# Queries and keys of twelve heads by two nested levels of seven block products, for both batch elements at once

## The chip, the cores and the metric

The kernel runs on one core of a Trainium2 chip. The metric is the device time of one execution in microseconds (us), as the median of several runs. Engines are named as the profile names them: PE (TensorE, matrix products; PEld is its weight load), DVE (VectorE), ACT (ScalarE), POOL (GpSimd) and SP, the queue from which nearly all DMAs are issued.

## The reference

A decoder layer in float32 on two batch elements of 512 tokens with 512 features. It has self-attention, cross-attention, a gated feed-forward part, and a layer normalisation after each.

```python
# self-attention: 16 heads of 128; the weights are FP4 codes with a scale per 32 rows
q = x @ (wq_codes * rows(wq_scales)) + bq          # k and v likewise
scores = einsum('bqhd,bkhd->bhqk', q, k) / sqrt(128)
out = einsum('bhqk,bkhd->bqhd', softmax(scores), v)
x = layernorm(x + out @ (wo_codes * rows(wo_scales)) + bo)
# cross-attention on 1024 context rows, of which the 54 best scores are kept
scores = where(scores < top_k(scores, 54)[..., -1:], -inf, scores)
x = layernorm(x + (softmax(scores) @ ctx) @ W_o.T)
# feed-forward: 512 -> 2 x 2048 -> 512
x = layernorm(x + (silu(gate) * up) @ w_down.T)
```

## The kernel before

**Block products.** Most products are done by a seven-product scheme for 2 x 2 blocks in place of eight: sums and differences of the blocks are formed first (`combine_a` for the stationary side, `combine_b` for the moving side, four operations each), then seven products run on TensorE, and their results are added up. `seven` does this for one block product: it numbers its products 1 to 7, gathers products 1, 6 and 7 in one PSUM bank `r`, from which ScalarE keeps three copies `u` (with the bias), and products 2, 4, 5, 3 in a two-bank PSUM tile `z`. Two VectorE operations form the results: `on_second` reads `z` and `u` before product 3 runs, `on_first` after it. The rest of a `seven` (product 3 and `on_first`) is left open, and is closed inside the next one. There are two buffers of `r`, two of `z` and two of one-bank tiles of the tag `t`; the scores of a head take both `z`.

**Units and phases.** A unit is one head of one element: 32 units. A phase is a group of four heads (`GH = 4`) of one element: eight phases. A phase has one product block for its values (`values`, two `seven`), one for its part of the output projection (`project`, two `seven`, added to the residual), and its four units. Before the change the first four heads are done for both elements, then the rest of the first element, then the rest of the second:

```python
phases = [(0, 0), (0, 1)] + [(g, b) for b in range(B) for g in range(1, NG)]
half_way = (NG + 1) * GH
```

**A unit.** `queries_keys(u)` makes queries and keys by one `seven` with 14 products of 128x256 (seven, two chunks of 128 features each). `weights(u)` computes the scores (four 128x512 products), the row maxima on VectorE, exponentials and scaling on ScalarE, a 32x32 transpose of four tiles on VectorE into `tq`, and then sixteen DMAs from SP that finish the transpose into `pt`. `attend(u)` multiplies `pt` by the values. In the main loop, step `i` makes queries, keys and weights of unit `i + 2` and attends unit `i`.

**Weights.** Codes and scales of a head's queries and keys are loaded (`load_qk`, `load_scales`), multiplied on GpSimd (`dequantise`, two pieces) and combined (`combine_qk`); values and output weights likewise. There are three buffers of scales (`sc0` to `sc2`). Apart from the first four heads, a head's weights are loaded and prepared once for each element.

**The search.** When the first element's self-attention is over (step `half_way`), its normalisation, the turning of its rows (`turn_x`), its cross-attention queries (`xquery`) and scores (`xscores`, steps `XS`) are worked into the second element's steps. The search for the 54th best score (`clips`) is a chain of maxima and replacements on VectorE, four of whose steps are written into each unit from `half_way + 4`.

**Order.** The order of each engine's instructions is made when the program is built. A scheduler takes the instructions by priority, which is the order of the program text, and lets a later one pass when an earlier one isn't ready by its own clock. On the chip each engine then follows its list.

Of the kernel before, what the change touches and what calls it, by code (L numbers as in the profile page):

```python
# [16 lines left out]
P = 128  # L17
# [7 lines left out]
def decoder_layer(  # L25
# [42 lines left out]
    sb = ctx.enter_context(tc.tile_pool(name="sb", bufs=1))  # L68
    ps = ctx.enter_context(tc.tile_pool(name="ps", bufs=2, space=PSUM))


# [173 lines left out]

    def load_residual():

        bo_sb = place("mt0", (D,), "bo_sb")
        nc.sync.dma_start(out=bo_sb, in_=bo.to_broadcast([P, D]))
        for b in range(B):  # L250
            rb[b] = place(f"res{b}", (NT, D), f"res{b}")
            nc.sync.dma_start(out=rb[b], in_=x[b].rearrange("(t p) d -> p t d", p=P))
            for t in range(NT):
                res[b, t] = rb[b][:, t, :]
                nc.gpsimd.tensor_tensor(res[b, t], res[b, t], bo_sb, ALU.add)
# [391 lines left out]

    phases = [(0, 0), (0, 1)] + [(g, b) for b in range(B) for g in range(1, NG)]
    units = [(g, b, j) for g, b in phases for j in range(GH)]
    half_way = (NG + 1) * GH  # L650
    last = len(phases) - 1

    def owner(p):
        return 0 if p == 1 else p

    def place_of_qk(u):

        return (u if u < GH else (u - GH) % 5) if u < half_way else (1, 2, 0)[(u - half_way) % 3]

    qkw, vw, ow, ks, qs, pts, vs, ots, raw = {}, {}, {}, {}, {}, {}, {}, {}, {}  # L660
    parts = {}
    scale_count = [0]

    def load(key, tag, shape, source, scales):

        w = place(tag, shape, "w" + key)
        if source is not None:
            nc.sync.dma_start(out=w, in_=source)
        raw[key] = (w, scales)

    def load_scales(key, n, queue):
        w, scales = raw[key]
        at, sv = scales[n]
        part = w if at is None else w[:, at, :]
        sct = place(f"sc{scale_count[0] % 3}", tuple(part.shape[1:]), f"s{key}_{n}")
        scale_count[0] += 1
        queue.dma_start(out=sct, in_=sv)
        parts[key, n] = (part, part, sct)
# [32 lines left out]
    def combine_qk(eng, u):  # L711
        w = raw[f"qk{owner(u // GH) * GH + u % GH}"][0]
        qkw[u] = combine_a(eng, blocks_pair(w), place(f"wc{u % 2}", (4, HK, P), f"wc{u}"))

    def combine_v(eng, p):
        w = raw[f"v{owner(p)}"][0]
        vw[p] = combine_a(eng, blocks_t(w), place("cmb0", (4, HK, GW // 2), f"vc{p}"))

# [17 lines left out]
    def queries_keys(u):  # L736

        g, b, j = units[u]
        h = g * GH + j
        qt = place(f"q{u % 2}", (2, HS), f"q{u}")  # L740
        kt = place(f"k{u % 2}", (2, HS), f"k{u}")
        seven(
# [8 lines left out]
        )  # L751
        qs[u], ks[u] = qt.rearrange("p n s -> p (n s)"), kt.rearrange("p n s -> p (n s)")

    def first_queries_keys():

        z = double("zqk0", (2, S))
        for k in range(KD):
            for c, n in ((c, n) for c in range(NT) for n in range(2)):
# [8 lines left out]
                )  # L767
        qs[0] = place("q0", (S,), "q0")
        ks[0] = place("k0", (S,), "k0")
        nc.scalar.activation(qs[0], z[:, 0, :], AF.Identity, bias=bq_sb[:, 0:1])  # L770
        nc.scalar.activation(ks[0], z[:, 1, :], AF.Identity, bias=bks[:, 0:1], scale=HSCALE)

    def weights(u):

        q, k = qs.pop(u), ks.pop(u)
        tq = place(f"tq{u % 2}", (NB, NT, NT, BLK), f"tq{u}")
        for t in range(NT):
            if t % 2 == 0:
# [7 lines left out]
                for n in range(2):  # L786
                    nc.tensor.matmul(  # L787
                        pair[n],
                        q[:, (t + n) * P : (t + n + 1) * P],
                        k,  # L790
                        start=True,
                        stop=True,
                    )
# [63 lines left out]
    def combine_o(eng, p):  # L857
        w = raw[f"o{p}"][0]
        ow[p] = combine_a(eng, blocks_t(w), place("wv" if p == last else "cmb1", (4, GH // 2, HD), f"oc{p}"))

    def project(p):

        g, b = phases[p]
        lo, hi = ots.pop((p, 0)), ots.pop((p, 1))
        oc = combine_b(
            nc.vector if p == last else nc.gpsimd,
            (lo[:, :, :HS], lo[:, :, HS:], hi[:, :, :HS], hi[:, :, HS:]),
            place("cmb0", (4, GH // 2, HS), f"otc{p}"),
        )
        rr = rb[b].rearrange("p (h s) (c f) -> p h s c f", h=2, c=2)  # L870
        for s in range(NT // 2):

            def add(z, u, s=s, c=1):
# [9 lines left out]
                oc,  # L883
                ow[owner(p)],
                slice(s * P, (s + 1) * P),
# [51 lines left out]
    combine_qk(nc.gpsimd, 2)  # L937
    dequantise(nc.gpsimd, "qk3")
    load_o(0)
    load_scales("o0", 0, nc.sync)  # L940
    load_scales("o0", 1, nc.sync)
    dequantise(nc.gpsimd, "o0", 0)
    dequantise(nc.gpsimd, "o0", 1)
    combine_o(nc.gpsimd, 0)


    due = {}
    for p in range(2, len(phases)):
        for j in range(GH):
            due.setdefault(p * GH + j - 1, []).append((f"qk{p * GH + j}", 0))  # L950
        for n in range(2):
            due.setdefault(p * GH - 3 + n, []).append((f"v{p}", n))
            due.setdefault((p * GH + 3 if p < last else p * GH + 2) + n, []).append((f"o{p}", n))

# [7 lines left out]
    lag = 2  # L962
    for i in range(len(units)):
        g, b, j = units[i]
        u = i + lag
        if u < len(units):
            gu, bu, ju = units[u]
            if ju == 0:
                values(u // GH)
            queries_keys(u)  # L970
            for key, n in due.get(u, []):
                dequantise(nc.gpsimd, key, n)
                if key == f"qk{u + 1}":
                    combine_qk(nc.gpsimd, u + 1)
                    if ju == GH - 1:
                        combine_v(nc.gpsimd, (u + 1) // GH)
                if key[0] == "o" and n == 1:
                    combine_o(nc.gpsimd, int(key[1:]))
            if u + 1 < 2 * GH:
                combine_qk(nc.gpsimd, u + 1)  # L980
                if u + 1 == GH:
                    combine_v(nc.gpsimd, 1)
        p = i // GH
        if j == 0 and 0 < p < last:
            project(p - 1)
            if p > 1:
                load_o(p)
        if i == len(units) - 2:
# [5 lines left out]
        if u < len(units):  # L994
            weights(u)
            if i == last * GH - 1:
                load_o(last)
            if 2 * GH <= u + 3 < len(units):
                load_qk(u + 3)
            if ju == 0 and 1 < u // GH + 1 < len(phases):  # L1000
                load_v(u // GH + 1)
            for key, n in due.get(u + 1, []):
                load_scales(key, n, nc.sync)
        if i == 0:
            load_residual()
            combine_x(nc.gpsimd, 1, "x0")
        if i == 2 * GH:
            load_memT(0)
# [74 lines left out]
    def up(b, half, eng, search=iter(()), between=iter(()), other=None, at=None):  # L1083
# [25 lines left out]
        for n in range(NH):  # L1109
# [10 lines left out]
            if other and n == (NH - 1 if at is None else at):  # L1120
                for _ in search:
                    pass
                for _ in other:
                    if sums:
                        sums.pop()()
            ut = place(f"k{n % 2}", (2, HS), f"ut{i}_{b}")
            uts[:] = [ut]
# [5 lines left out]

            def first(z, u, i=i, n=n, ut=ut, ht=hs[n]):
                gt = place(f"q{n % 2}", (2, HS), f"gt{i}_{b}")
                nc.vector.tensor_add(gt, z, u)  # L1136
# [175 lines left out]
```

## Time and profile before

| | |
|---|---|
| median of 3 runs | 1082.58 us (1081.91 to 1083.0) |
| the profiled execution | 1082.82 us, span 1081.0 us |
| mean granted TensorE clock | 0.998 |
| PE busy | 1070.0 us (99%), 4300 instructions |
| DVE busy | 610.9 us (57%) |
| POOL busy | 574.3 us (53%) |
| ACT busy | 409.0 us (38%) |
| DMA | 142.72 MB, mean 132 GB/s |

A product in float32 appears as two PE instructions, so `x8` in a row of the profile is four products. PE's busy time is modelled from its instructions' lengths; how far apart their starts are tells more. A group's row ends with the engine's idle time ahead of its instructions and what ended it.

### The profile page before, as it was taken

The page shows a single profiled execution, that of the slowest core. Times are in us where ns is not written, and L with a number is a line of the kernel's source. Part 1 is how long each engine was busy: PE and PEld are TensorE (multiplying, and loading weights), DVE is VectorE, ACT ScalarE, POOL GpSimd, SP SyncE. Part 2 cuts the span into 40 slices and gives each one's busy share as a digit, 9 for nine tenths or more (in the row PEclk, how much of TensorE's full clock was granted, in tenths as well). Part 3 has the DMA queues.
Part 4 walks back from the last instruction along what each step waited for, and adds up shares of the span by engine and source line. Part 5 has one row for each costly group of instructions (what it writes and reads, how often), then busy time and mean ns, then how long its engine had stood idle before and what let it go on. Part 6 is the DMA issues. An engine that isn't in the chain of part 4 may idle for free.

```text
span 1081.0 us, 12892 instructions
## 1 busy us (share of the span) xinstructions
PE 1070.0 (99%) x4300; PEld 801.8 (74%) x4300; DVE 610.9 (57%) x1015; ACT 409.0 (38%) x882; POOL 574.3 (53%) x578
## 2 busy tenths in 40 slices
PE   9999999999999999999999999999999999999997
PEld 7676776677677677665666567778888888888886
DVE  5444334334434435643898774468999736554254
ACT  3445335335344533733444353222443214221221
POOL 4965636846845846514852654525565712264530
PEclk9999999999999999999999999999999999999999
DMA  9545456554663555635442537331324401522201
GB/s 349 160 106 175 156 137 222 178 162 143 192 195 95 175 170 156 196 81 180 136 117 78 146 109 253 88 108 39 97 66 131 136 21 49 166 82 78 96 19 39
DMA packets 66258, 142.72 MB, mean 132 GB/s; under 512 B 12560, under 2 KB 12560, under 8 KB 66192
## 3 DMA queue, kind: packets, MB, share of 16 engines
q1 hardware_dynamic: 65472, 140.32, 42.4%
q10 hardware_dynamic: 720, 1.57, 0.4%
q8 instruction: 35, 0.57, 0.2%
q14 instruction: 31, 0.25, 0.1%
HBM read 99.90 MB, written 2.10 MB: 94 GB/s over the span
## 4 chain that ended last, share of the span: by engine, by line
PE 83%; DVE 13%; ACT 2%; POOL 1%; issue 1%; DMA 0%; DVEq 0%; ACTq 0%; POOLq 0%
PE sc L787 10%; PE av L832 9%; PE zqk L187 9%; PE rqk L187 7%; PE zgu L187 7%; PE zo L187 5%; PE rgu L187 5%; PE zv L187 5%; PE zpd L187 4%; PE ro L187 4%; DVE work L493 4%; PE rv L187 3%; DVE top L496 3%; PE rpd L187 3%; PE zxav L187 3%; PE xs L474 2%
## 5 line engine op out<-in xcount | busy, mean ns | idle before, releaser
L798 DVE TENSOR_REDUCE nm<-sc 128x2 f32<-128x1024 f32 x63 | 77.0, 1223 | 80.1 <-PE sc L787 80.1
L832 PE MATMUL av<-pt,v 128*128 128x512 f32 x256 | 121.6, 592 | 0.0
L787 PE MATMUL sc<-k,q 128*128 128x512 f32 x256 | 117.1, 598 | 0.0
L801 ACT ACTIVATE p<-sc,nm 128x512 f32<-128x512 f32 x128 | 86.9, 681 | 76.0 <-DVE nm L798 75.9
L812 DVE STREAM_TRANSPOSE tq<-p 128x512 f32<-128x512 f32 x128 | 84.9, 699 | 36.9 <-ACT p L809 30.7
L787 PEld LDWEIGHTS sc<-k,q 128*128 128x128 f32 x256 | 47.3, 190 | 62.2 <-issue 51.3
L107 POOL TENSOR_TENSOR wc<-wgu 128x256 f32<-128x256 f32 x32 | 25.4, 794 | 114.8 <-PE zgu L187 70.9
L809 ACT ACTIVATE p<-p,sm 128x512 f32<-128x512 f32 x128 | 85.4, 715 | 1.6 <-DVE sm L808 1.4
L684 POOL TENSOR_TENSOR wqk<-wqk,sqk 128x512 f32<-128x512 f32 x52 | 66.0, 1286 | 35.9 <-DMA wqk<-in_wqk 20.4
L197 ACT ACTIVATE ugu<-rgu 128x256 f32<-128x256 f32 x96 | 36.3, 379 | 103.1 <-PE rgu L187 100.8
L832 PEld LDWEIGHTS av<-pt,v 128*128 128x128 f32 x256 | 48.6, 190 | 30.9 <-issue 27.3
L187 PE MATMUL rgu<-x2c,wc 128*128 128x256 f32 x256 | 66.1, 380 | 1.0 <-ACT ugu L197 1.0
L187 PE MATMUL rqk<-x0c,wc 128*128 128x256 f32 x248 | 65.0, 384 | 0.1
L496 DVE MAX8 top<-work 128x8 f32<-128x1024 f32 x48 | 58.6, 1222 | 0.9
L850 ACT ACTIVATE ot<-av,bqkv_sb 128x512 f32<-128x512 f32 x28 | 19.2, 687 | 102.4 <-PE av L832 102.4
L187 PEld LDWEIGHTS rgu<-x2c,wc 128*128 128x128 f32 x256 | 48.3, 190 | 8.7 <-ACT ugu L197 1.6
L187 PEld LDWEIGHTS rqk<-x0c,wc 128*128 128x128 f32 x248 | 45.1, 189 | 12.0 <-ACT uqk L197 4.4
L1136 DVE TENSOR_TENSOR gt<-zgu,ugu 128x512 f32<-128x512 f32 x32 | 21.9, 684 | 48.4 <-PE zgu L187 48.4
L493 DVE MATCH_REPLACE8 work<-top,work 128x1024 f32<-128x1024 f32 x40 | 48.4, 1209 | 0.0
L879 POOL TENSOR_TENSOR res<-res,uo 128x512 f32<-128x512 f32 x24 | 30.7, 1278 | 31.7 <-DVE res L877 27.7
L107 POOL TENSOR_TENSOR wc<-wqk 128x256 f32<-128x256 f32 x31 | 22.6, 731 | 46.4 <-PE zqk L187 46.3
L116 POOL TENSOR_TENSOR otc<-ot 128x512 f32<-128x512 f32 x7 | 8.9, 1268 | 66.5 <-PE zv L187 66.5
(313 smaller groups left out, 2469.1 us busy)
## 6 DMA issues: line engine op xcount, KB each, us to landing
pt<-tq SPq DMA_DIRECT2D x512, 64.0 KB, 2.0
wgu<-in_wgu SPq DMA_DIRECT2D x32, 512.0 KB, 3.4
wqk<-in_wqk SPq DMA_DIRECT2D x26, 512.0 KB, 5.7
sqk<-in_wqk_s SPq DMA_DIRECT2D x26, 512.0 KB, 4.3
wdn<-in_wdn SPq DMA_DIRECT2D x8, 1024.0 KB, 5.5
sv<-in_wv_s SPq DMA_DIRECT2D x14, 512.0 KB, 6.2
wv<-in_wv SPq DMA_DIRECT2D x7, 1024.0 KB, 5.5
wo<-in_wo SPq DMA_DIRECT2D x7, 1024.0 KB, 5.8
```

The costliest lines, as they stand in the source:

```text
L107: eng.tensor_tensor(c[0], a10, a11, ALU.add)
L187: nc.tensor.matmul(o, left[k][:, cols], right[k], start=start and k == 0, stop=k == len(left) - 1, skip_group_check=not start,)
L197: nc.scalar.activation(u[:, i, :], r, AF.Identity, bias=at, scale=scale)
L493: nc.vector.match_replace(work, top, src, LOWEST)
L496: nc.vector.max(top, work)
L684: eng.tensor_tensor(part[:, w], codes[:, w], sct[:, w], ALU.mult)
L787: nc.tensor.matmul(pair[n], q[:, (t + n) * P : (t + n + 1) * P], k, start=True, stop=True,)
L798: nc.vector.reduce_max(nms, scs, axis=AX.X, negate=True)
L801: nc.scalar.activation(pr, pair[t % 2], AF.Exp, bias=nms[:, t % 2 : t % 2 + 1], accum_out=sm,)
L809: nc.scalar.activation(pr, pr, AF.Copy, scale=sm)
L812: nc.vector.transpose(tq[:, :, :, t, :].rearrange("p n k c -> p k n c"), pr.rearrange("p (k n a) -> p k n a", n=NB, a=BLK),)
L832: nc.tensor.matmul(av, vs[u // GH][:, k, j * P : (j + 1) * P], pt[:, :, k, :], start=(k == 0), stop=(k == NT - 1),)
```

## The change

The order of the phases becomes all of the first element, then the second element's groups 1, 2, 3 and 0; `half_way` is 16. For the twelve heads of groups 1 to 3, queries and keys of two heads and of both elements are made in one joint product while the first element is at work. The blocks of the scheme are then themselves multiplied by the scheme: for each of the seven outer products an inner scheme of seven products, whose blocks are two chunks of features by two heads (stationary) and by two elements (moving). That makes 49 products of one chunk for two heads and two elements, where four units had 56.

- `inner_x` forms the inner sums of x on VectorE (28 operations of 128x256), once. They take the rooms `mt0`, `mt1` and `res1`, and the second element's block sums are changed in place; so x of the second element is loaded and combined again after the last joint product.
- `inner_first` and `inner_sums` form the weights' inner sums on GpSimd. `inner_sums` comes after the previous joint product.
- `Inner` is the inner scheme; `joint(n)` interleaves the seven of pair `n` and adds their results up on VectorE in `outer`, 28 operations of 128x512, some of which read one PSUM and one SBUF operand, the others two SBUF operands.
- The second element's queries and keys go to HBM (`joint_store`) and come back (`load_stored`) one to two units ahead of their use. So the second element's phases of groups 1 to 3 have no query-key products, loads or sums of their own; group 0 of the second element has, and its weights are loaded again.
- In the stretch of the joint products `tq` has one buffer (the other holds the second head's queries and keys), and loads and stores are pinned into program order on SP (`pin`).
- `project_sums` is taken out of `project`, and is called earlier where the joint products are.

```diff
-    phases = [(0, 0), (0, 1)] + [(g, b) for b in range(B) for g in range(1, NG)]
+    phases = [(g, 0) for g in range(NG)] + [((g + 1) % NG, 1) for g in range(NG)]
     units = [(g, b, j) for g, b in phases for j in range(GH)]
-    half_way = (NG + 1) * GH
+    half_way = NG * GH
...
+    def inner_x():
...
+            c0, c1, c3 = next(free), next(free), next(free)
+            eng.tensor_tensor(c0, b01, b00, ALU.subtract)
+            eng.tensor_tensor(c1, b11, c0, ALU.subtract)
+            eng.tensor_tensor(b01, b11, b01, ALU.subtract)
+            eng.tensor_tensor(c3, b10, c1, ALU.subtract)
...
+    class Inner:
...
+        def on_second(self):
+            self.second(self.z[:, 0::2, :], self.u[:, 2:3, :].to_broadcast([P, 2, HS]))
+
+        def p3(self):
+            self.mm(3, self.z[:, 2, :], False)
+            self.first(self.z[:, 1:3, :], self.u[:, 0:2, :])
+
+    def joint(n):
...
+        def outer(o, x, z, c):
+            em, q0, q1, k0, k1 = e[:, x], qf[x][:, 0], qf[x][:, 1], kf[x][:, 0], kf[x][:, 1]
+            if o == 1:
+                add(em, z, c)
+            elif o == 2:
+                add(q0, z, c)
+                add(q0, q0, em)
+            elif o == 4:
+                add(k0, z, c)
+            elif o == 6:
+                add(em, em, c)
+                add(em, z, em)
+                add(k0, k0, em)
+            elif o == 5:
+                add(q1, em, c)
+                add(q1, z, q1)
+            elif o == 7:
+                stt(k1, z, HSCALE, c, ALU.mult, ALU.add)
+                stt(k0, k0, HSCALE, k1, ALU.mult, ALU.add)
+                stt(k1, q1, HSCALE, k1, ALU.mult, ALU.add)
+            else:
+                add(q1, q1, c)
+                add(q1, z, q1)
...
+        for m in range(2, len(sevens) + 1):
+            s, r, q = (sevens[k] if k < len(sevens) else None for k in (m, m - 1, m - 2))
+            if s:
+                s.p1()
+            q.p3()
+            r.p7()
+            r.p5()
+            r.p4()
+            r.on_second()
+            if s:
+                s.p6()
+            r.p2()
+            yield
...
+    for n in range(NP):
+        i, u = 2 + 2 * n, GH + 2 * n
+        more = n + 1 < NP
+        if more:
+            scales(f"qk{u + 2}")
+            scales(f"qk{u + 3}")
+        p = n // 2
+        for m, _ in enumerate(joint(n)):
+            if m == 0 and n % 2 == 0:
+                for k in range(2):
+                    dequantise(nc.gpsimd, f"o{p}", k)
+            if more and m == 1:
+                dequantise(nc.gpsimd, f"qk{u + 2}")
+                dequantise(nc.gpsimd, f"qk{u + 3}")
...
+            if more and m == 3:
+                inner_first(nc.gpsimd, n + 1)
+        attend(i)
+        joint_store.pop()()
+        weights(u)
+        if more:
+            inner_sums(nc.gpsimd, n + 1)
...
+        if n % 2 == 0:
+            values(p + 1)
+            combine_o(nc.gpsimd, p)
...
+        else:
+            project(p)
...
+        attend(i + 1)
+        weights(u + 1)
...
+    for i in range(half_way - lag, len(units)):
...
-            queries_keys(u)
+            if u >= last * GH:
+                queries_keys(u)
```

## The prediction

> **What bounds the kernel now.** I read the page's first table, then a table of windows for the stages, then the chain of waits, then the groups by shape, and last the timeline of the DMA queue.
>
> ```profile
> span 1081.0 us, 12892 instructions
> PE 1070.0 (99%) x4300; PEld 801.8 (74%) x4300; DVE 610.9 (57%) x1015; ACT 409.0 (38%) x882; POOL 574.3 (53%) x578
> ```
>
> The table of windows (columns: width, busy PE, PEld, DVE, ACT, POOL, clock, DMA share, GB/s):
>
> ```profile
> 80.00:432.00 352.00, 352.00 (x1319) 246.93 (x1318) 155.09 (x263) 149.82 (x344) 218.82 (x209) 1.00 0.55 165
> 530.00:650.00 120.00, 118.99 (x398) 74.05 (x397) 97.26 (x151) 58.27 (x119) 66.00 (x56) 1.00 0.39 108
> ```
>
> TensorE is never idle in the first element's phases, at full clock, with VectorE at 44% and GpSimd at 62%. In the stretch where the clipping search runs, VectorE is at 81%. So products taken away shorten the kernel one for one, as far as the other engines keep up. The chain shows what a product costs, and how PE's order hides waits (start, us, what, count of PE instructions):
>
> ```profile
> 86.64 3.43 PE sc L787 x8
> 90.08 0.86 PE rqk L187 x4
> 90.94 0.86 PE av L832 x2
> 91.80 1.73 PE zqk L187 x8
> 684.18 3.45 PE zxav L187 x16
> ```
>
> One 128x256 instruction takes 3.45/16 = 0.2156 us, a product of one chunk (two instructions) 0.431, a score or attend block (eight) 3.43. The two "av" instructions stand between parts of a query-key product: where the product waits for the scores' softmax, the order fills in an older head's attend.
>
> **Removed: 18.1 us of TensorE.** A unit (head and element) has 7 products of 2 chunks, 14. Two heads and two elements have 56; the joint form has 49. Six pairs of heads lose 42 products, 84 instructions: 84 x 0.2156 = 18.1 us. Attend, scores, values and projections keep their counts. It also removes, off the path, the second loading of 12 heads and 24 dequantising pieces of 1.286 us on GpSimd.
>
> **Added in the joint products, on VectorE.** Counted from `outer`: 28 VectorE operations of 128x512 for a pair, where four units had 8. Fourteen read PSUM, fourteen read SBUF twice. The rows that price them:
>
> ```profile
> L684 POOL TENSOR_TENSOR wqk<-wqk,sqk 128x512 f32<-128x512 f32 x52 | 66.0, 1286 | 35.9 <-DMA wqk<-in_wqk 20.4 <-DMA sqk<-in_wqk_s 11.9 <-DMA pt<-tq 3.3
> L496 DVE MAX8 top<-work 128x8 f32<-128x1024 f32 x48 | 58.6, 1222 | 0.9
> L493 DVE MATCH_REPLACE8 work<-top,work 128x1024 f32<-128x1024 f32 x40 | 48.4, 1209 | 0.0
> L748 DVE TENSOR_TENSOR q<-zqk,uqk 128x512 f32<-128x512 f32 x31 | 21.3, 688 | 39.3 <-PE zqk L187 39.3
> L1103 DVE TENSOR_TENSOR hc<-h 128x256 f32<-128x256 f32 x12 | 9.9, 823 | 0.0
> L118 DVE TENSOR_TENSOR otc<-ot_last 128x512 f32<-128x512 f32 x1 | 1.8, 1764 | 0.0
> L118 DVE TENSOR_TENSOR x2c<-x2T 128x512 f32<-128x512 f32 x2 | 1.4, 684 | 0.0
> ```
>
> At 0.69 each they take 19.3 us. From the last scores before a joint product to the first after it, PE has 49 x 0.431 + 3.43 (attend) = 24.5 us. VectorE has the softmax part of the last unit (two maxima of 1.22, four transposes of 0.66, four reciprocals of 0.15: 5.7) and 19.3: 25.0 us. They are level, so the joint stretch alone has no cover. What can be put into it is the other work of the pair: the second attend (3.43) and values or projection (28 x 0.431 = 12.1). Over a whole pair PE has 21.1 + 4 x 3.43 + 12.1 = 46.9 us, VectorE 19.3 + 2 x 5.7 + 2.8 = 33.5.
>
> The two-input operations can cost more. The last two rows are the same subtraction, 684 ns with GpSimd idle and 1764 beside two of its sums; L1103 takes 823 ns beside GpSimd's sums of the down weights, where its shape takes 424 alone: 0.40 more in the mean. GpSimd has, for a pair, two heads' dequantising (5.1), first sums (eight of at most 0.73, half of them half as long: 4.8), second sums (11.1 from rows of 0.73 and 1.27), and half a phase of values and output weights (15.3): 36.3 of 46.9 us. It falls unevenly: the scales of the next pair are pinned on SP behind the last unit's 16 transposing DMAs, so GpSimd is busy in the joint products that follow a projection and free for much of the others. With 55% on average, 14 x 0.40 x 0.55 = 3.1 us a joint product. Since half the pair's PE work can stand in, I let a third reach PE: 1.0 us, 6.2 in six. The ends: 0, if the order hides it; and 14 x 0.40 x 0.77 + 0.5 = 4.8 each, 29 in all, if nothing does. Less than nothing is excluded, as PE's pitch is already counted.
>
> [...]
>
> At the start of a joint product its second read-out on ScalarE stands behind four exponentials and scalings (0.68 and 0.72 each), about 4 us. The "av" rows show such a wait filled, and one attend and more is ready: I take 0; the other end, 4 x 6 = 24, goes to the first rival.
>
> **Moved: the second element's first three phases have no query-key products.** Two consequences. First, the weights' way to attend:
>
> ```profile
> 163.33 3.60 PE L787 MATMUL sc<-k,q 128*128 128x512 f32 x8
> 173.31 23.20 SPq L820 DMA_DIRECT2D pt<-tq  x32
> 569.15 10.01 SPq L820 DMA_DIRECT2D pt<-tq  x16
> pt<-tq SPq DMA_DIRECT2D x512, 64.0 KB, 2.0
> ```
>
> The last score instruction starts at 163.33 + 7 x 0.43 = 166.3, the first DMA 7.0 later; sixteen take 10.0 to issue and 2.0 to land: 19.0 us. Cover is now values or projection, an attend and a score block: 12.1 + 3.4 + 3.4 + 0.4 = 19.4, where it had 12 more. In a pair with 6.9 us between its scores the second one's DMAs queue 3.1 behind the first's, 2.7 too late. That can hit units 17 and 19 (later ones have cross-attention queries and scores behind them): 5.4. PE can do the next unit's scores first, their operands come by DMA: I take 1, ends 0 and 5.4. The loads of stored queries and keys go behind the same 16 DMAs, and have over 20 us.
>
> Second, the search. Four tiles x (seven maxima, six replacements with their 0.08 loads, one 1.55 product) = 71.4 us. It is written for seven units, i = 20 to 26. There VectorE also has 7 x 5.7 and 12.6 of additions: 124 us. PE has 7 x 6.87 + 4 x 12.1 + 3 x 6.87 + 6.0 = 123 us, where before the same seven units had about 150. At i = 24 and 25 VectorE has 34.4 against 25.8. Search steps can go forward into i = 20 and 21 (39.5 of PE): I take 2.5, ends 0 and 8.6.
>
> **Small ends.** Before the first joint product VectorE gets the second element's sums (4 x 0.68) and inner sums of x (28 x 0.42), 14.6 us in a stretch where it is half idle; GpSimd's list there grows by 16 and ends just in time: 1, ends 0 and 5. After the last joint product x of the second element is loaded again (about 8 us), summed (5.1) and its values' weights too (5.1), within about 24 us of PE: 1, ends 0 and 6. Stores through HBM (24 DMAs) go to a queue that has 47 us a pair for about 26 (32 x 0.63 and a dozen others of 0.4): 0; if they held up the next unit's DMAs, under 1 each. The last projection now adds on GpSimd: 0, hidden by the cross-attention products; 2 without.
>
> Sum: -18.1 + 6.2 + 1 + 2.5 + 1 + 1 = -6.4. The profiled execution took 1082.82 (span 1081.0 and 1.8 around it), 0.24 above the median of the runs: 1082.58 - 6.4 = 1076.2.
>
> **Rivals.** (a) Slower: VectorE sets the pace of the joint products. Place: PE waits for the second result's additions before each third product. From 3.0 us each it eats the 18.1. [...] Against: half of the pair's PE work can stand in. At 4.8 each, with the small terms: -18.1 + 29 + 5.5 = +16, 1099; at 3.5 each +8, 1091; part of the bubble at the start would count as well. (b) Slower: joint products as forecast, but the second element's phases run at VectorE's and the queue's pace: -18.1 + 6.2 + 5.4 + 8.6 + 6 + 1 = +9, 1092. Against: search and scores can move. (c) Everything hidden: 1064.5; for it, TensorE's order lost only about 0.3 us in 25 in the first element's phases. That the change does not remove the products is excluded: the loops are fixed in the code.
>
> **How the numbers follow.** Forecast 0.32 (0.04 of it within 0.2%, which is 2.2 us, about what a measurement can tell from no change), (c) 0.24, (a) 0.25 (0.02 within), (b) 0.15, other 0.04, halved. Faster 0.54, same 0.06, slower 0.40. The range goes from (c) to just under (a) at its full price: 1064 to 1098. The forecast's own is 1069 to 1082.
>
> **What would show it.** 4216 matmul records, give or take a few missing; PE's idle time inside the joint products near 1 us each (over 3: (a)); two-input additions near 0.9 us in the mean (0.69: hidden; over 1.1: (a)); attends of units 17 and 19 waiting for a landing under 1 us each; PE waiting for maxima in i = 24 to 26 under 4 us. The forecast falls if these sum to 16 or more.

## The result: 5.5% slower, and the profile after

The changed kernel took 1141.53 us (median of 4 runs, 1140.34 to 1145.02) against 1082.79 for the kernel before in the same measurement (1081.91 to 1083.33): a ratio of 1.0549, 95% interval 1.0523 to 1.0574. The forecast was 1076.2, and the range ended at 1098. The profiled execution of the changed kernel took 1142.41 us, with a span of 1140.6.

The first table of its page:

```profile
span 1140.6 us, 13032 instructions
PE 1078.0 (95%) x4216; PEld 788.8 (69%) x4216; DVE 739.3 (65%) x1167; ACT 427.6 (37%) x936; POOL 618.1 (54%) x598
```

The products went as the diff says: 4300 - 4216 = 84 instructions. But TensorE, 99% busy before, is 95% busy of a longer span. The table of windows shows where (width, busy PE, PEld, DVE, ACT, POOL, clock, DMA share, GB/s); the first row is the stretch of the joint products:

```profile
80.00:380.00 300.00, 276.64 (x1032) 192.35 (x1030) 213.03 (x296) 122.86 (x294) 219.82 (x201) 0.98 0.47 143
530.00:650.00 120.00, 116.89 (x377) 70.69 (x375) 105.62 (x168) 59.56 (x124) 61.79 (x50) 1.00 0.54 167
```

In the joint products TensorE is idle for 23 of 300 us, VectorE has gone from 44% to 71%, and the granted clock is 0.98 where it was 1.00. In the stretch of the search TensorE stays nearly full although VectorE is at 88%.

Busy time is modelled, so I used the starts for the account: for every pair of neighbouring TensorE instructions, the time from start to start beyond the pitch of its shape (0.216 us for 128x256, 0.429 for 128x512). I call the sum of a stage its excess; idle time and time at a lower clock are both in it.

| Excess, us | before | after | more |
|---|---|---|---|
| start, to the first joint product (67 us; before, to 68) | 3.9 | 16.3 | 12.4 |
| joint products (67 to 380; before, 68 to 392) | 4.2 | 42.8 | 38.6 |
| from there to the cross-attention queries (380 to 500.6; before, 392 to 488.4) | 2.3 | 19.5 | 17.2 |
| second element's phases with the search (500.6 to 709; before, 488.4 to 650) | 3.3 | 12.4 | 9.1 |
| rest | 4.9 | 5.4 | 0.5 |
| sum | 18.6 | 96.4 | 77.8 |

77.8 less the 18.1 of the products taken away is 59.7; the spans differ by 59.6. So the whole loss is in this table, and it has four places.

**The joint products.** The chain of waits after, where before it had only products, runs through VectorE in the middle of a joint product (start, us, what, count):

```profile
205.38 1.68 DVE qa L891
207.05 1.68 DVE qkb L891
209.57 1.75 PE zj L828 x4
```

TensorE's instructions around it; the brackets hold the idle time before and who ended it:

```profile
209.57 0.89 PE L828 MATMUL zj<-x0c,wc 128*128 128x256 f32 x2 [2.77 <-DVE qkb L892]
...
214.81 1.02 PE L1039 MATMUL av<-pt,v 128*128 128x512 f32 x2
215.67 1.46 PE L188 MATMUL rv<-wv,x0T 128*128 128x256 f32 x6
```

GpSimd's at the same time, sums of the next values' weights:

```profile
206.58 1.59 POOL L109 TENSOR_TENSOR vc<-vc,wv 128x512 f32<-128x512 f32 x1
208.25 1.59 POOL L111 TENSOR_TENSOR vc<-wv,vc 128x512 f32<-128x512 f32 x1
```

And SP's, the transposing DMAs of the attend that could have filled the wait (start, time to issue all sixteen):

```profile
192.58 14.12 SPq L1027 DMA_DIRECT2D pt<-tq  x16
```

Two additions of `outer` on two SBUF operands follow each other 1.68 us apart, side by side with GpSimd's sums of 1.59, and the product behind them waits 2.77. The work that the prediction had put under this wait is not there: the attend's last transposing DMA is issued at 206.7 and needs some 2.0 us to land (the median of these DMAs), and the first value products, whose weights were dequantised at 204.8, stand behind it in TensorE's list. The groups by shape show which additions are long:

```profile
L887 DVE TENSOR_TENSOR e<-e,uj 128x512 f32<-128x512 f32 x12 | 12.4, 1034 | 2.4 <-ACT uj L831 2.3
L895 DVE SCALAR_TENSOR_TENSOR ka<-ka 128x512 f32<-128x512 f32 x6 | 8.6, 1441 | 0.1
L891 DVE TENSOR_TENSOR qkb<-e,uj 128x512 f32<-128x512 f32 x6 | 7.3, 1215 | 0.0
L892 DVE TENSOR_TENSOR qkb<-zj,qkb 128x512 f32<-128x512 f32 x6 | 4.1, 690 | 0.4
L688 POOL TENSOR_TENSOR wqk<-wqk,sqk 128x512 f32<-128x512 f32 x36 | 50.0, 1414 | 31.4 <-DMA sqk<-in_wqk_s 31.4
```

Additions that read `zj` in PSUM take 0.69 us, those of two SBUF operands 0.83 to 1.44 by line, and 1.095 in the mean of all 84; the 84 that read PSUM have a mean of 0.685. Sorted by what GpSimd did meanwhile, the 84 fall apart: 26 ran while it was idle and took 0.688 in the mean, 50 ran while it was at work (over 90% of their time) and took 1.319, and 8 lie between (by the trace's spans, which are rough for GpSimd). GpSimd pays too: its dequantising piece was 1286 ns before, and is 1414 now.

**The start.** TensorE waits for the read-out of the values' products (TensorE's row first, then VectorE's), which stands behind the inner sums of x on VectorE. Of the 28 inner sums, 13 ran while GpSimd was idle (0.41 us in the mean) and 15 beside its work (0.92):

```profile
44.08 3.78 PE L994 MATMUL sc<-qk 128*128 128x512 f32 x4 [3.69 <-DVE v L735]
```

```profile
39.69 1.48 DVE L773 TENSOR_TENSOR x0T<-x0T 128x256 f32<-128x256 f32 x1
41.09 1.48 DVE L774 TENSOR_TENSOR xi<-x0T,xi 128x256 f32<-128x256 f32 x1
...
43.35 0.68 DVE L735 TENSOR_TENSOR v<-zv,uv 128x512 f32<-128x512 f32 x1
```

**Before the cross-attention queries.** The longest wait of the kernel, in TensorE's and in SP's list. Unit 19's sixteen DMAs start at 468.83:

```profile
485.52 5.81 PE L1039 MATMUL av<-pt,v 128*128 128x512 f32 x8 [7.13 <-DMA pt<-tq]
```

```profile
454.69 12.43 SPq L1027 DMA_DIRECT2D pt<-tq  x16
...
468.34 0.38 SPq L374 DMA_DIRECT2D wq<-in_xwq  x1
468.83 15.15 SPq L1027 DMA_DIRECT2D pt<-tq  x16
```

They stand behind unit 18's, which take 12.4 us to issue in place of 10.0, and behind three loads, the last of them the query weights of the cross-attention; they then take 15.2 themselves. And the attend that follows takes 5.81 us for its eight instructions, where the eight of the scores behind it, at a granted clock of 1.00, take 3.60. Before the change, the context's columns were loaded in the middle of the first element's phases:

```profile
169.00 0.94 SPq L356 DMA_DIRECT2D memT<-in_memT  x2
```

In the changed kernel their rooms `mt0` and `mt1` hold inner sums of x until the last joint product, so these two loads are called at step `half_way - 1` and go out at 386.1 and 450.1, the second of them ahead of unit 18's DMAs. The stage's other waits are 2.20 us for GpSimd's sums of the values' weights, and 1.13 and 2.40 for exponentials on ScalarE.

**The last phase** waits for GpSimd's weights, whose scales were issued late:

```profile
649.06 1.13 PE L188 MATMUL rqk<-x0T,wqk 128*128 128x256 f32 x4 [0.98 <-POOL wqk L688]
```

```profile
647.73 2.50 POOL L688 TENSOR_TENSOR wqk<-wqk,sqk 128x512 f32<-128x512 f32 x2 [8.55 <-DMA sqk<-in_wqk_s]
```

TensorE's waits for GpSimd's weights in this phase come to 3.7 us. No run tried this place.

### The profile page after: what moved, and what is told of

Read it like the earlier page. It is cut to its first block, busy times and chain, and to the rows that moved or that the text cites. A ratio compares the mean times of both kernels' runs of the same rounds, so it can differ in the third digit from the quotient of the medians.

```text
span 1140.6 us, 13032 instructions
## 1 busy us (share of the span) xinstructions
PE 1078.0 (95%) x4216; PEld 788.8 (69%) x4216; DVE 739.3 (65%) x1167; ACT 427.6 (37%) x936; POOL 618.1 (54%) x598
## 4 chain that ended last, share of the span: by engine, by line
PE 57%; DVE 24%; DMA 6%; ACT 4%; POOL 3%; issue 3%; SPq 3%; ACTq 0%; DVEq 0%; POOLq 0%
PE zgu L188 7%; PE av L1039 6%; PE sc L994 6%; PE rgu L188 5%; PE zpd L188 4%; PE zj L828 4%; DVE work L494 3%; PE zv L188 3%; PE zo L188 3%; PE rpd L188 3%; DVE top L497 3%; PE rj L828 3%; PE rv L188 2%; PE zxav L188 2%; PE ro L188 2%
## 5 line engine op out<-in xcount | busy, mean ns | idle before, releaser
L1019 DVE STREAM_TRANSPOSE tq<-p 128x512 f32<-128x512 f32 x128 | 84.2, 694 | 25.4 <-ACT p L1016 22.3
L108 POOL TENSOR_TENSOR wc<-wgu 128x256 f32<-128x256 f32 x32 | 25.6, 800 | 116.6 <-PE zgu L188 72.1
L994 PE MATMUL sc<-qk 128*128 128x512 f32 x160 | 74.7, 607 | 4.6 <-DVE v L735 3.7
L688 POOL TENSOR_TENSOR wqk<-wqk,sqk 128x512 f32<-128x512 f32 x36 | 50.0, 1414 | 31.4 <-DMA sqk<-in_wqk_s 31.4
L688 POOL TENSOR_TENSOR wv<-wv,sv 128x512 f32<-128x512 f32 x28 | 38.1, 1384 | 48.0 <-DMA sv<-in_wv_s 32.7
L688 POOL TENSOR_TENSOR wo<-wo,so 128x512 f32<-128x512 f32 x32 | 44.0, 1400 | 36.2 <-DMA so<-in_wo_s 36.2
L994 PEld LDWEIGHTS sc<-qk 128*128 128x128 f32 x160 | 30.5, 193 | 42.4 <-issue 33.0
L1443 DVE TENSOR_TENSOR gut<-zgu,ugu 128x512 f32<-128x512 f32 x32 | 21.9, 684 | 48.3 <-PE zgu L188 48.3
L831 ACT ACTIVATE uj<-rj 128x256 f32<-128x256 f32 x72 | 27.3, 385 | 44.0 <-PE rj L828 28.2
L1092 DVE TENSOR_TENSOR res<-zo,res 128x512 f32<-128x512 f32 x32 | 21.8, 683 | 20.4 <-PE zo L188 20.2
```

Source lines behind the costliest of these rows:

```text
L688: eng.tensor_tensor(part[:, w], codes[:, w], sct[:, w], ALU.mult)
L994: nc.tensor.matmul(pair[n], q[:, (t + n) // 2, (t + n) % 2 * P : ((t + n) % 2 + 1) * P], k, start=True, stop=True,)
L1019: nc.vector.transpose(tq[:, :, :, t, :].rearrange("p n k c -> p k n c"), pr.rearrange("p (k n a) -> p k n a", n=NB, a=BLK),)
```

## The experiments

My theory: VectorE paces the joint products because its additions of two SBUF operands are long beside GpSimd's work, and the other three places lose time by themselves, each for its own reason. The rivals: the joint form itself (its count of VectorE instructions, its read-outs on ScalarE) is too slow whatever an addition costs; the new order of the phases is what costs; or one engine paces everything, so that what is gained at one place is lost at the next. Ratios are against the kernel before, on the same chip.

**Without the two-input additions.** Of `outer`, only the fourteen operations that read PSUM are left.

```diff
             elif o == 2:
                 add(q0, z, c)
-                add(q0, q0, em)
...
-                add(em, em, c)
-                add(em, z, em)
-                add(k0, k0, em)
+                add(em, z, c)
```

> Leaves out the fourteen VectorE operations of a joint product that read SBUF twice (each result block keeps one addition that reads PSUM). Products, GpSimd's work and DMAs stay. Theory A (VectorE sets the pace of the joint products): the waits of TensorE between 68 and 392 us of the span, 43 us in the changed kernel, fall under 12 and the time from 1141 to about 1108. Theory B (the waits come from the chain of read-outs on ScalarE and the two PSUM buffers): they stay above 30, time above 1128.

Measured: 1113.07 us, ratio 1.0269 (1.0250 to 1.0288). The excess of the joint products falls from 42.8 to 14.4, and that of the other places stays (16.4, 18.4, 11.7). That is close to theory A, and a little short of its 12 and 1108. So these 84 additions, with 92 us of VectorE's time, cost 28.4 of the 38.6 us; another 10.2, 1.7 a joint product, is there without them. In this run's trace the 10.2 are ten waits (5.8 us of excess) and more of the short stalls of under 0.2 us that the kernel before has too (8.6 us for 4.2).

**The same additions with GpSimd quiet.** In the joint stretch, dequantising and the inner sums of the query and key weights are left out (fills that only write take the place of some); all 28 operations of `outer` run.

```diff
     def dequantise(eng, key, n=0):
         part, codes, sct = parts.pop((key, n))
+        if pinned[0]:
+            return
...
-            inner_sums(nc.gpsimd, n + 1)
+            inner_sums(None, n + 1)
```

> Leaves out most of GpSimd's work in the stretch of the joint products (dequantising, and the weights' inner sums of pairs 1 to 5; a fill that only writes takes their place); VectorE's work is whole. [...] Theory A2 (28 operations are too many for VectorE even alone): operations at 0.70, waits above 28, time above 1125.

Measured: 1119.46, ratio 1.0334 (1.0315 to 1.0353); excess of the joint products 20.5. The mean of the 84 falls to 0.826; some work is left on GpSimd (its busy time goes from 618 to 479 us). The group that took 1215 ns:

```profile
L898 DVE TENSOR_TENSOR qkb<-e,uj 128x512 f32<-128x512 f32 x6 | 5.2, 864 | 0.3 <-ACT uj L838 0.3
```

So it is GpSimd's company that made the additions long (how it does so is not shown by any run): 84 x (1.095 - 0.826) = 22.6 us of VectorE's time go with it, and 22.3 of the 38.6 us, though no VectorE instruction of the joint products was removed. Of TensorE's 23.9 us of waits there in the changed kernel, none ended with a result of GpSimd's, so what went isn't TensorE's waiting for weights. Neither the count of VectorE's instructions nor the scheme's shape is then the main cost. Both measures stay short of what I expected if GpSimd's company were all of it (0.70 to 0.75 us, waits under 15).

**Without the inner sums of x.** The four subtractions of `inner_x` are left out, and their rooms are filled with a constant.

```diff
             c0, c1, c3 = next(free), next(free), next(free)
-            eng.tensor_tensor(c0, b01, b00, ALU.subtract)
-            eng.tensor_tensor(c1, b11, c0, ALU.subtract)
...
```

> Leaves out the 28 inner subtractions of x on VectorE before the first joint product (their rooms are filled once). Theory: they, beside GpSimd, cost the first 68 us their extra 12 us of TensorE waits; without them these waits fall from 16 to about 5 and the time to about 1130. Rival: the second element's block sums (moved to VectorE) and GpSimd's longer list cost it; then at least 10 us of waits stay, time above 1136.

Measured: 1133.39, ratio 1.0464 (1.0447 to 1.0481). Excess of the start 8.5 for 16.3; the two waits for `v` (2.45 and 3.69 us) are gone. That lies between the two expectations. 4.6 more than before are left, with a wait of 1.85 for ScalarE as the longest; what causes them was not tried.

**Loads from ScalarE's queue.** In the second element's phases, the loads of weights, scales and stored queries and keys, the context columns and the query weights are issued by ScalarE, so that SP has the transposing DMAs alone.

```diff
+    loadq = [nc.sync]
...
-            pin(nc.sync.dma_start(out=w, in_=source))
+            pin(loadq[0].dma_start(out=w, in_=source))
...
     pinned[0] = False
+    loadq[0] = nc.scalar
```

> From step 14 on the loads (weights, scales, stored queries and keys, context, cross-attention weights) are issued from ScalarE's queue; the transposing DMAs keep SP's. Theory C (the head of the line on SP: a unit's 16 DMAs stand behind the unit before and behind bulk loads): the 7.1 us wait of an attend is gone, waits of TensorE from 392 to 530 us fall from 20 to under 8, those from 640 to 720 from 8.5 to under 5, time about 1124. Rival (late softmax on VectorE and ScalarE, or landing bandwidth): the wait stays above 4 us, time above 1134.

Measured: 1158.01, ratio 1.069 (1.0673 to 1.0707): it lost 16.5 us more, and the expectation failed. The excess before the cross-attention queries rose from 19.5 to 31.0, that of the phases after it from 12.4 to 19.1. ScalarE's list shows why:

```profile
428.18 0.33 ACTq L682 DMA_DIRECT2D so<-in_wo_s  x1
428.56 0.69 ACT L1009 ACTIVATE p<-sc,nm 128x512 f32<-128x512 f32 x1 [9.11 <-POOL wv L689]
```

A load into a buffer that GpSimd has yet to free holds the exponentials behind it for 9.11 us. The run doesn't tell whether SP alone would have been fast enough, so the question was put again in the run without bulk loads.

**The additions through PSUM.** The whole computation. Where `outer` added two SBUF operands, the first sum is now written into the bank of `z` that was just read, and the second addition reads it from there: 12 two-input operations are left of 84, and VectorE has as many operations as in the change.

```diff
             elif o == 2:
-                add(q0, z, c)
-                add(q0, q0, em)
+                add(t, z, c)
+                add(q0, t, em)
...
             elif o == 5:
-                add(q1, em, c)
-                add(q1, z, q1)
+                add(t, z, c)
+                add(q1, t, em)
```

> The whole computation, with the same number of VectorE operations: the middle sums of a joint product (block plus kept copy) are written back to PSUM, so that twelve of the fourteen operations that read SBUF twice read one PSUM and one SBUF operand. [...] Theory A2 (28 operations alone set the pace, or the longer hold of PSUM costs as much as it gives): waits above 33, time above 1131.

Measured: 1128.1, ratio 1.0413 (1.0390 to 1.0436), 13.4 us faster than the change, and between the 1119 that I expected if the additions' length were all of it and the 1131 of theory A2. In the groups by shape, the addition of the diff's last line, which now reads its first sum from PSUM:

```profile
L892 DVE TENSOR_TENSOR qa<-zj,e 128x512 f32<-128x512 f32 x6 | 4.1, 687 | 0.1
```

The 156 operations that read PSUM have a mean of 0.689, whether they write PSUM or SBUF. The excess of the joint products falls to 25.6 (and rises by 4.3 before the cross-attention queries; the cause of that was not tried), not to the 14.4 of the first run, though VectorE's price is mended: the bank of `z` is now held until its second addition, and TensorE's waits there are ended by ScalarE's read-outs (5.1 us) and exponentials (4.0). That the held bank causes these waits is inferred, not tested.

**The order alone.** This is the kernel before with the changed order of the phases, `half_way` 16, and the buffers' turns that go with it; every unit makes its own queries and keys. In one point it isn't the whole computation: for the second phase, GpSimd forms the sums of the values' weights (from 46.3 us) before the weights' second half has its scales (79.1 us), so that phase's values are wrong. The count of TensorE's instructions is that of the kernel before; in the right order these sums would come later still, so the time is no exact price of the order.

```diff
-    phases = [(0, 0), (0, 1)] + [(g, b) for b in range(B) for g in range(1, NG)]
+    phases = [(g, 0) for g in range(NG)] + [((g + 1) % NG, 1) for g in range(NG)]
-    half_way = (NG + 1) * GH
+    half_way = NG * GH
```

> The kernel before with the new order of phases alone: the first element's heads first, the second's group 0 last; no joint products, every unit makes its own queries and keys, all weights are loaded for each element. Theory C (the second element's phases wait because the products that covered the softmax and its DMAs are gone): waits of TensorE from 380 us to the cross-attention queries stay under 5, time within 6 us of the kernel before (1083). Rival (the order itself, its earlier normalisation and search, costs): over 8 us slower than before.

Measured: 1107.76, ratio 1.0232 (1.0217 to 1.0248): this order by itself loses about 25 us, but at other places than the change does. About 20 of it lie between 60 and 125 us, where the second phase now wants its own weights. Of 12.2 us of waits there, 5.3 end with GpSimd's weights, the others with read-outs on ScalarE and VectorE:

```profile
72.15 1.97 PE L187 MATMUL rv<-vc,x0c 128*128 128x256 f32 x4 [3.17 <-ACT uv L197]
...
109.42 1.70 PE L187 MATMUL rqk<-x0c,wc 128*128 128x256 f32 x4 [2.15 <-POOL wc L108]
```

Its excess before the cross-attention queries is 0.6, where the change has 19.5. So the waits there don't come from the order: they come with the joint form. That is two things at once, phases without query-key products of their own, and the context's columns loaded at this place; in this run they are loaded at 221.7 us.

**Without the bulk loads.** The context columns and the query weights of the first element (3 loads of 1 MB) are not loaded but set to a constant.

```diff
-        nc.sync.dma_start(out=xw[name], in_=w.rearrange("(k p) f -> p k f", p=P))
+        if name == "wq" and b == 0:
+            nc.gpsimd.memset(xw[name], 0.01)
+        else:
+            nc.sync.dma_start(out=xw[name], in_=w.rearrange("(k p) f -> p k f", p=P))
```

> Leaves out the loads of the first element's context for the scores (two of 1 MB) and of its cross-attention query weights (1 MB); fills take their place. Theory C1 (bulk loads ahead of the 16 DMAs on SP hold them up): the longest wait of an attend falls from 7.1 to under 3 us, waits from 380 us to the cross-attention queries from 19.5 to about 13. Theory C2 (it is the 16 DMAs of the unit before, and the softmax): the wait stays above 5.

Measured: 1135.38, ratio 1.0496 (1.0476 to 1.0515). The wait of 7.13 us before unit 19's attend is 1.10, the stage's excess 10.6 for 19.5, and the sixteen DMAs of units 18 and 19 take 10.46 and 10.04 us. So most of that wait, 6.03 of 7.13 us, goes with the bulk loads; whether they take it in SP's queue or by their transfers, the run doesn't part.

**The wait filled.** Sixteen products of zeros before the attend of unit 19, to keep TensorE busy in the wait.

```diff
+        if i == half_way + 3:
+            warm = bank("t", "warm")
+            for _ in range(16):
+                tc.keep_in_program_order(
+                    nc.tensor.matmul(warm[:, :HS], zero[:, :P], zero, start=True, stop=True)
+                )
```

> Adds sixteen products of zeros (6.9 us) ahead of the attend that waits 7.1 us in the changed kernel, in TensorE's order. Theory D (TensorE's clock halves after an idle stretch of some us): the clock stays at 1.0 there, that attend's eight instructions take 3.4 us in place of 5.7, and the waits up to the cross-attention queries fall by 2 to 4 us; time 2 to 4 us less. Rival (the slow instructions come from something else that ends the wait): they stay at 5.7, time the same or longer.

Measured: 1140.95, ratio 1.0536 (1.0519 to 1.0553). TensorE's list:

```profile
478.52 7.07 PE L1303 MATMUL warm<-zero 128*128 128x256 f32 x32
487.53 3.67 PE L1039 MATMUL av<-pt,v 128*128 128x512 f32 x8 [1.94 <-DMA pt<-tq]
```

The attend that took 5.81 us, at a granted clock of 0.50 up to 489.84, takes 3.67, so the half clock came from the wait. The expected gain in time didn't come; it changed by less than the interval: the landing came 2 us later in this execution, and scores and output products that wait for ScalarE (1.12 and 2.40) stand behind.

**Three causes left out at once**: the edits of the runs without two-input additions, without inner sums and without bulk loads, together.

> Leaves out at once what e1, e3 and e7 left out one by one: the joint products' additions of two SBUF operands, the inner sums of x, and the two bulk loads (context columns and query weights of the first element, set to a constant). Alone they gave back 28.5, 8.1 and 6.2 us of the changed kernel's 1141.5. Theory (three separate places, each on the path by itself): the gains add, 1141.5 - 42.8 = 1098.7, between 1095 and 1103, and still slower than the kernel before, since the waits behind GpSimd's weights late in the kernel (about 9 us of excess beyond pitch against 3) and about 1.5 us a joint product remain. Rival (one pacing engine, so that a gain at one place is lost at the next): 1108 or more.

Measured: 1097.59, ratio 1.0148 (1.0133 to 1.0163). 1141.53 less the three single gains (28.46, 8.14, 6.15) is 1098.8. The gains add, so these are separate places, not one engine that hands its delay on. The excess that is left, by the stages of the table (start 7.3, joint products 14.4, before the queries 10.5, after them 13.0, rest 5.3; 50.5 in all) is 31.9 above that of before, against the 18.1 us of products.

**The whole computation, both mends.** The sums through PSUM, and the query weights and context columns loaded behind the sixteen DMAs of unit 19.

```diff
-        if i == half_way - 1:
-            load_memT(0)
         if i == half_way:
-            load_xw("wq", xwq, "cmb1")
...
         if i == half_way + 1:
+            pinned[0] = True
+            load_xw("wq", xwq, "cmb1")
+            pinned[0] = False
...
             turn_x(0, "xc0", "xT0", "x1T")
+            pinned[0] = True
+            load_memT(0)
+            pinned[0] = False
```

> The whole computation. The sums of e5 (written to PSUM, 1128.1 us), and the first element's query weights and context columns are loaded behind the sixteen transposing DMAs of unit 19 in place of between those of units 17 to 19. Theory (the bulk loads in the same queue delay the attend of units 18 and 19): the wait of 7 us before unit 19's attend goes to under 2 and the half clock after it too; gain 4 to 9 us, 1119 to 1124. Rival (the landing only moves): the cross-attention queries then wait for their weights, and the time stays within 2 us of 1128. Both expect it slower than the kernel before.

Measured: 1122.07, ratio 1.0373 (1.0356 to 1.0390), 6.0 us faster than the sums through PSUM alone. The sixteen DMAs of units 18 and 19 are back at their price:

```profile
440.65 10.01 SPq L1027 DMA_DIRECT2D pt<-tq  x16
...
451.90 10.32 SPq L1027 DMA_DIRECT2D pt<-tq  x16
```

Unit 19's attend waits 0.50 us, and 2.09 of the gain is given back where the cross-attention queries wait for the turned rows. It is the fastest whole version of the joint form that I ran, and it is 40 us slower than the kernel before. None beat that kernel.

## Why the prediction was wrong, step by step

| Term, us | predicted | measured |
|---|---|---|
| products taken away | -18.1 | -18.1 |
| joint products | +6.2 | +38.6 |
| inner sums of x at the start | +1 | +12.4 |
| units 17 and 19, and x loaded again | +2 | +17.2 |
| search, and the last phase | +2.5 | +9.1 |
| rest | 0 | +0.5 |
| sum | -6.4 | +59.7 |

**The products** were right: 4216 records, and the account closes with 0.2156 us for each of 84.

**The joint products: the step that failed is "I let a third reach PE".** Two sizes in it were off. A two-input addition was put at 0.69 + 0.40 x 0.55 = 0.91; it took 1.095, so that the extra is 0.41 x 14 = 5.7 us a joint product in place of 3.1. Both factors were too small. The 0.40 came from a row of operations half as long, and the dearest of four such rows (L1103 at 823 ns; L1105 to L1107 took 458 to 561); with GpSimd at work all the while, an addition of this length took 1.319 - 0.688 = 0.63 more. The 0.55 was an estimate of GpSimd's share in the joint products; 50 of the 84 additions had it at work all the while and 8 in part. And not a third of the extra time reached TensorE: with GpSimd quiet, VectorE had 22.6 us less to do and the excess fell by 22.3, nearly all of it. (The run without these additions takes away their plain 0.69 too, so its 28.4 can't be set against the extra 34.4.) The reserve, "half of the pair's PE work can stand in", was counted but not placed: the attend's transposed weights land in the middle of the joint product, and the values stand behind it in TensorE's list. That the scheduler's clock knew nothing of the longer additions would explain such a list; no run shows it. The prediction's own sums had the warning, in the level balance of 25.0 against 24.5 us.

Rival (a) was the right mechanism, in the right place, and the run with GpSimd quiet confirms it. Its price of 4.8 a joint product is close to what the two-input additions cost by the run without them, 28.4 / 6 = 4.7; that is partly luck, as its extra was 0.40 x 0.77 = 0.31 an addition, where 0.41 was measured. The joint products cost 6.4 each: 1.7 was there without these additions, where the prediction had taken 0 for the wait at a joint product's start, with an end of 4. What causes that 1.7 was not tried.

On VectorE itself the prediction had 84 x 0.40 x 0.55 = 18.5 us more; measured are 84 x 0.41 = 34.4. An addition took 0.689 us with an operand in PSUM (the run with the sums through PSUM), 1.095 with both in SBUF, and 0.826 with GpSimd quieter. Over the 50 additions that had GpSimd at work all the while, the extra was 0.63 us; the mean is lower because 26 of the 84 met GpSimd idle.

**The start**: the mechanism was named, the size was off. 28 inner sums were priced at 0.42 us, 11.8 in all, in a stretch "where it is half idle". They took 0.69 in the mean, 0.38 to 1.48 (0.41 with GpSimd idle, 0.92 beside its work), and the read-out of the values was behind them in VectorE's list. The end given, 5, was passed too: 12.4.

**Units 17 and 19**: the 19.0 us against a cover of 19.4 took sixteen DMAs at 10.0 us. With the bulk loads in the same queue they took 12.4 and 15.2. The prediction counted the loads of stored queries and keys behind the DMAs, but not the 1 MB loads for the cross-attention; two of the three were moved to this place by the change itself, as the inner sums of x hold their rooms. By the runs, the loads in the queue are 6.0 to 6.2 us of the time. What the rest of the stage's 17.2 comes from was not tried.

**The search** was overrated: between 530 and 640 us the excess is 3.1 against 2.9. What the stage lost lies after it, at 640 to 709 us (7.9), where the last phase's dequantising waited 8.6 us for scales; the prediction had no term for it, and no run tried it.

**Not foreseen at all: the clock.** The sum took every wait at its length. In the changed kernel's trace there are seven stretches, 30.7 us in all, at a granted clock of 0.50; in the trace of before there is one only from 1077.72 us, after its last product (1075.00). In these stretches instructions of 128x256 start 0.427 us apart in place of 0.216, those of 128x512 0.854 in place of 0.429, so about half of the busy time in these stretches, some 13 us (an estimate: 30.7 less about 4 idle, halved), is part of the 77.8.

**The marks** that were to show it: records 4216 (met); idle time over 3 us a joint product, so (a) (23.9 us of waits in six, 4.0 each; 6.4 of excess); two-input additions 1.095, just below the 1.1 set for (a); the attend of unit 19 waiting 7.13 for under 1. The condition set for the forecast's fall, a sum of 16 or more, was passed by the joint products alone. Every term but the search's erred to the same side. I read that as one error, though no run shows it as one: each was given a price from a stretch in which TensorE was always fed, and the change takes away the very products that fed it.

## What to carry to other kernels

Where an engine's new load is level with the engine that it serves, count no reserve that isn't placed: for every piece of stand-in work, work out when its operands land and where it stands in the list. Price an operation beside the work that will run beside it: here a VectorE addition with both operands in SBUF took 1.319 us beside GpSimd's work and 0.688 without, and one with an operand in PSUM 0.685 either way. Products that are taken away also hid DMAs; list what was under them, the loads of other stages too.

## What the runs showed of the hardware

**The granted clock fell to 0.50 after waits of TensorE.** In the changed kernel's record of the granted clock, the stretches at 0.50 start at 35.87, 42.70, 162.16, 209.95, 326.00, 483.01 and 500.08 us; the second and the sixth last 6.83 us, the others 3.41. The steps between the starts are 2, 35, 14, 34, 46 and 5 times 3.413 us. I summed TensorE's idle time in pieces of 3.413 us laid out from these starts. In the piece ahead of each stretch it was 2.41, 2.30, 2.25, 2.77, 1.77, 3.41 and 2.40 us. Of the pieces that no half clock followed, those with the most had 1.96 us (from 312.35) and 1.80 (from 267.97). So in this trace one wait of 2.40 us (before 499.40), which lies within one piece, was followed by half clock, and one of 2.76 us (before 316.56), which lies in two, was not. The window after the wait for unit 19 shows what it costs (the columns are those of the windows above):

```profile
486.40:489.80 3.40, 3.40 (x5) 1.33 (x4) 0.00 (x0) 0.00 (x0) 0.00 (x0) 0.50 0.89 325
```

TensorE is busy for the whole window. Five 128x512 instructions lie in it in part or whole; four start in it, 0.854 us apart, where 3.40/0.429 gives eight.

**An addition into PSUM cost VectorE no more than one into SBUF** (0.69 us both, 128x512, in the run with the sums through PSUM).

**Additions of two SBUF operands were slow beside GpSimd's work, and not with it idle.** In the changed kernel such an addition of 128x512 took 0.688 us with GpSimd idle (26 of them, 0.679 to 0.694) and 1.319 in the mean with GpSimd at work all the while (50, 0.675 to 1.780); one with an operand in PSUM took 0.685 either way (28 with GpSimd idle, 51 with it at work).

**Sixteen transposing DMAs took 12.4 and 15.2 us of SP's queue with loads of 1 MB issued just ahead of them** (units 18 and 19 in the changed kernel); with those loads behind them they took 10.0 and 10.3, and 10.5 and 10.0 without the loads.
